# The end of layer 1: ring-buffer operands, sums of two chunks on four column groups, and the order of the projection halves

## The chip, the cores and the metric

The kernel runs on one core of a Trainium2 chip. The metric is the time of one execution on the device in microseconds (us), the median of several runs. A profiled execution also has a span, from its first to its last recorded instruction. The engines are named as in the profile: PE is TensorE (PEld its weight loads), DVE is VectorE, ACT is ScalarE, POOL is GpSimd, SP is SyncE, which here only issues DMAs; "SPq" and "ACTq" rows are DMA issues by SP and ACT.

## The reference, cut to what matters

Two layers work on an array of 2 x 256 x 64 x 64 float32 numbers. Layer 0 is a normalised attention with a gate, and the change doesn't touch it. Layer 1 is softmax attention with four heads of 64 over 4096 positions, an output projection, a bias and a residual:

```
qkv = einsum('oc,bchw->bohw', w_qkv, x) + b_qkv
q, k, v = split(qkv.reshape(b, 4, 192, h*w), 3, axis=2)
attn = softmax(einsum('bhdn,bhdm->bhnm', q, k) / sqrt(64), axis=-1)
out = einsum('bhnm,bhdm->bhnd', attn, v).reshape(b, c, h, w)
return einsum('oc,bchw->bohw', w_out, out) + b_out + x
```

The reshape takes the (4096, 64) result of a head as it lies in memory for 64 rows of 4096. So 512 positions of a head are 8 whole rows of the projection's input, and the projection of any block of 512 columns needs some rows from every block of positions.

## The kernel before

Layer 1 (`L750` on) is cut into 32 units `(b, g, j)`: batch, pair of heads, block of 512 queries. A unit has 32 chunks of 128 keys, in two groups of 16 (`GS`). For each chunk PE makes the scores of both heads (`score`, L878: 128 x 1024 in PSUM), DVE keeps a running maximum (L895) and ACT copies the scores to a ring of 26 SBUF buffers `raw` (`keep`, L896). When a group is through, its maxima are turned by PE (`turn_max`, L903), reduced by DVE (`fold`, L920), written to DRAM as `neg` and read back, spread over all partitions, as `row` (L923, L927). ACT puts the row in PSUM (`place_shift`, L940). From then on, 11 steps (`LAG`) behind the scores, DVE adds the shift to each chunk (`shift`, L948), ACT takes the exponential (`weigh`, L960), and PE multiplies with the values into `av` (`gather`, L982). The sums of the exponentials are made by POOL, one addition to `acc` a chunk (L972); in the last 22 chunks of all (`on_tensor`) most chunks are summed by PE instead, with a product by ones for each single chunk (L992, into `late_sums`). Chunks 10, 11, 12 and 13 of the last unit and all later odd ones go to PE.

A step is two chunks. A list `extras` says what else is hung into a step, at which place in it (`start`, `early`, `early end`, `late`, `late end`, `end`). `seq` keeps the order of the compute instructions on each engine as the code emits them; DMAs on SP keep an order of their own, and each waits at the head of the queue for what it needs. `END` is the step after the last scores. What follows it, steps `END` to `END + 17`, is the drain: no scores any more, only shift, exponential and product of the last 22 chunks, then the last unit's rows.

The last unit's end is in this order. `total` (L1012) adds the POOL sums to `late_sums`. ACT copies them (`keep_total`, L1021), PE turns them (`turn_total`, L1049), POOL and DVE make the factors (L1059, L1060, L1066, L1067), PE turns the two groups' `av` copies (L1042), DVE and POOL make the rows (`rows`, L1077, L1084, L1088). The rows go to DRAM in `att` (L1094, one DMA from SP and one from ACT) and come back, 8 rows of 4096 each, as the last rows of `last_att` (L1100).

The output projection of the last batch is done in two halves of the contraction: half 0 with heads 0 and 1 (`att_first`, long done), half 1 with heads 2 and 3 (`last_att`). `project_half` makes for a block of 512 columns two products (L1231) into a pair of PSUM banks; DVE adds bias and residual after half 0 (L1237) and the rest after half 1 (L1241), both into `x_last`. Half 0 of blocks 0 to 7 is hung into steps of the drain by `FILL`: blocks 0, 1, 2 at its start, 3 to 7 after the last chunk. Half 1 follows for all eight blocks at the very end, each with its store (L1288). `last_output` (L1212) hands the ring's memory to a pool `tail` and loads into it the other rows of `last_att` (L1221) and blocks 5, 6, 7 of the residual `x_last` (L1225); so these loads wait until the ring is no longer used.

Of the kernel before, what the change touches and what calls it, by code (L numbers as in the profile page):

```python
# [14 lines left out]
P = 128  # L15
# [11 lines left out]
def conv_attention_kernel(  # L27
# [740 lines left out]
    with (  # L768
        tc.tile_pool(name="l1", bufs=2) as l1,
        tc.tile_pool(name="psp", bufs=2, space=PSUM) as psp,  # L770
# [4 lines left out]
        own_ring = ExitStack()  # L775
        ring = own_ring.enter_context(tc.tile_pool(name="ring", bufs=2 * LAG + 4))
# [23 lines left out]
        last_att = []  # L800
        first, begun = {}, set()
# [96 lines left out]
        def turn_max(u, n, k):  # L898

            b, g, j = u  # L900
            ps = misc(f"rt_{b}_{g}_{j}_{n}_{k}")
            for i in range(PB):
                seq(nc.tensor.transpose(  # L903
                    ps[:, bass.ts(i, P)], rmax[u, n][:, k, bass.ts(i, P)], ident
                ))
            rts[k] = ps
# [45 lines left out]
        def on_tensor(t):  # L952
            return t >= LATE and (t % 2 == 1 or t < LATE + 4)
# [19 lines left out]

        def gather(t):
# [11 lines left out]
            raws.pop(t - 1, None)  # L986
            if on_tensor(t):
                if u not in srows:
                    srows[u] = psp.tile([P, 2, NB], F32, tag="pair", name="late_sums")[:, 0, :]
                for k in range(2):  # L990
                    r = D1 * n + 32 * k
                    seq(nc.tensor.matmul(  # L992
                        srows[u][r : r + 32, :], ones[:, :32], raws[t][:, k, :],
                        start=r not in begun, stop=False, skip_group_check=True,
                    ))
                    begun.add(r)
# [5 lines left out]
        def total(u):  # L1002


            b, g, j = u
            late = u in srows
            if not late:
                srows[u] = misc(f"sum1_{b}_{g}_{j}")
            for n in range(NG):
                for k in range(2):  # L1010
                    r = D1 * n + 32 * k
                    seq(nc.tensor.matmul(  # L1012
                        srows[u][r : r + 32, :], ones[:, :32], accs[u, n][:, k, :],
                        start=not late, stop=True, skip_group_check=late,
                    ))

        def keep_total(u):
            b, g, j = u
            row = l1.tile([P, NB], F32, tag="kv", name=f"srow_{b}_{g}_{j}")
            if u == units[-1]:  # L1020
                seq(nc.scalar.copy(row, srows[u]))  # L1021
                seq(nc.scalar.activation(losts[u], losts[u], AF.Exp, scale=D1**-0.5))
                srows[u] = row
                return
# [20 lines left out]
        def turn_total(u):  # L1045

            ps = misc("sumt")
            for i in range(PB):
                seq(nc.tensor.transpose(ps[:, bass.ts(i, P)], srows[u][:, bass.ts(i, P)], ident))  # L1049
            s = small.tile([P, NG, 2, PB], F32, tag="sums1", name="sums1_last")  # L1050
            seq(nc.vector.tensor_copy(
                s.rearrange("p n k i -> p i (n k)"),
                ps.rearrange("p (i m e) -> p i m e", i=PB, e=32)[:, :, :, 0],
            ))
            srows[u] = s
# [17 lines left out]
        def rows(u, n):  # L1073
# [6 lines left out]
            last = u == units[-1]  # L1080
# [6 lines left out]
            engine = nc.vector if last else nc.gpsimd  # L1087
            seq(engine.tensor_tensor(r, r, halves.pop(u), ALU.add))  # L1088
# [3 lines left out]
            for k in range(2):  # L1092
                queue = (nc.sync, nc.scalar)[k if last else 0]
                queue.dma_start(  # L1094
# [3 lines left out]
                if last:  # L1098
                    c = ((2 * g + k) * N + j * NB) // D1
                    queue.dma_start(  # L1100
                        out=last_att[0][c % P : c % P + NB // D1, :],
                        in_=att[b][c : c + NB // D1, :],
                    )
# [40 lines left out]
        for n, u in enumerate(units):  # L1144
# [21 lines left out]
            for k in range(NG):  # L1166
                t1 = t0 + (k + 1) * GS // 2
                for i, place in enumerate(("early", "late")):
# [4 lines left out]
            at(t1 + 4, "early", lambda u=u: total(u))  # L1173
            at(t1 + 4, "early end", lambda u=u: keep_total(u))
            at(t1 + 1, "late", lambda u=u: lose(u))
            if u == units[-1]:
                at(t1 + 5, "early", lambda u=u: turn_total(u))
            at(t1 + 5, "late end", lambda u=u: add_sums(u))
            at(t1 + 7, "start", lambda u=u: factors(u))
            for place, k in (("early", 1), ("late", 0)):  # L1180
                at(t1 + 9, place, lambda u=u, k=k: turn_sums(u, k))
                at(t1 + 9, f"{place} end", lambda u=u, k=k: rows(u, k))
# [13 lines left out]
        last_x, first_half = [], []  # L1196

        def fetch_last(i):

            b = B - 1  # L1200
            tag, bufs, pool = (("xb", 3, l1x), ("xo", 1, l1), ("ao", 1, l1))[(i >= 3) + (i >= 4)]
            t = pool.tile([P, CC, NB], F32, tag=tag, bufs=bufs, name=f"x_last_{i}")
            nc.sync.dma_start(out=t, in_=x1[b][i].rearrange("(c p) n -> p c n", p=P))
            last_x.append(t)

        def fetch_first_half():
            for i in range(NJ):
                t = l1o.tile([P, NB], F32, tag=f"k{i}", name=f"att_first_{i}")
                nc.sync.dma_start(out=t, in_=att[B - 1][:P, bass.ts(i, NB)])
                first_half.append(t)  # L1210

        def last_output():  # L1212


            own_ring.close()
            tail = own_tail.enter_context(tc.tile_pool(name="tail", bufs=1))
            b = B - 1
            a = tail.tile([P, N], F32, tag="att", name="last_att")
            for k in range(2):
                r, n = k * D1, D1 - NB // D1  # L1220
                nc.sync.dma_start(out=a[r : r + n, :], in_=att[b][P + r : P + r + n, :])  # L1221
            last_att.append(a)
            for i in range(NJ - 3, NJ):
                t = tail.tile([P, CC, NB], F32, tag=f"xo{i}", name=f"x_last_{i}")
                nc.sync.dma_start(out=t, in_=x1[b][i].rearrange("(c p) n -> p c n", p=P))  # L1225
                last_x.append(t)

        def project_half(j, c, a):
            ps = psp.tile([P, 2, NB], F32, tag="pair", name=f"o1_{c}_{j}")
            for o in range(CC):  # L1230
                seq(nc.tensor.matmul(  # L1231
                    ps[:, o, :], wo1[:, c, bass.ts(o, P)], a, start=True, stop=True
                ))
            for o in range(CC):
                x = last_x[j][:, o, :]
                if c == 0:
                    seq(nc.vector.scalar_tensor_tensor(  # L1237
                        x, ps[:, o, :], bo1[:, o : o + 1], x, ALU.add, ALU.add
                    ))
                else:  # L1240
                    seq(nc.vector.tensor_tensor(x, ps[:, o, :], x, ALU.add))  # L1241

        own_tail = ExitStack()
        for i in range(NJ - 3):
            at(END - 11 + 2 * i, "start", lambda i=i: fetch_last(i))
        at(END, "start", lambda: fetch_first_half())
        at(END + LAG, "late end", lambda: last_output())


        FILL = {  # L1250
            (END, "early end"): (0,), (END + 1, "early"): (1,), (END + 2, "early"): (2,),
# [90 lines left out]
```

## Time and profile before

| what | us |
|---|---|
| median of 3 runs (4685.09 to 4686.68) | 4685.69 |
| the profiled execution's own time | 4685.7 |
| its span | 4683.7 |
| around the span | 2.0 |

| busy in the whole span | PE | DVE | ACT | POOL |
|---|---|---|---|---|
| us | 4505.0 | 3897.1 | 3429.8 | 2515.8 |
| share | 96% | 83% | 73% | 54% |

The shares of the whole span say little about the change, which concerns the last 95 us. What matters there is read from three views: busy time by stretch of the span, the chain of work that ended last (each row: start, duration, what it was), and the timeline (start, duration, engine, line, operation, tile written and read, count, and in brackets the idle time before it with what ended it). A float32 product of 512 columns appears as two records on PE.

### The profile page before, as it was taken

The page shows a single profiled execution, that of the slowest core. Times are in us where ns is not written, and L with a number is a line of the kernel's source. Part 1 is how long each engine was busy: PE and PEld are TensorE (multiplying, and loading weights), DVE is VectorE, ACT ScalarE, POOL GpSimd, SP SyncE. Part 2 cuts the span into 40 slices and gives each one's busy share as a digit, 9 for nine tenths or more (in the row PEclk, how much of TensorE's full clock was granted, in tenths as well). Part 3 has the DMA queues.
Part 4 walks back from the last instruction along what each step waited for, and adds up shares of the span by engine and source line. Part 5 has one row for each costly group of instructions (what it writes and reads, how often), then busy time and mean ns, then how long its engine had stood idle before and what let it go on. Part 6 is the DMA issues. An engine that isn't in the chain of part 4 may idle for free. (4 is left out here: it accounts for less than half of the span.)

```text
span 4683.7 us, 70880 instructions
## 1 busy us (share of the span) xinstructions
PE 4505.0 (96%) x27286; PEld 1512.7 (32%) x27286; DVE 3897.1 (83%) x4505; ACT 3429.8 (73%) x4587; POOL 2515.8 (54%) x1310
## 2 busy tenths in 40 slices
PE   8999999999999999989999999999999999999998
PEld 3433333333333333333333333333333333223222
DVE  6777777777777777449999999999999999999996
ACT  3366666666666666668888888888888888888884
POOL 5300000000000000009999999999999999999994
PEclk9999999999999999999999999999999999999999
DMA  3100000000000000121111221111211112211213
GB/s 100 39 4 20 19 20 15 15 15 17 15 15 15 15 13 13 44 72 35 39 37 39 59 46 39 33 41 43 68 39 38 38 37 64 52 46 39 48 46 99
DMA packets 199166, 174.70 MB, mean 37 GB/s; under 512 B 121124, under 2 KB 121956, under 8 KB 198700
## 3 DMA queue, kind: packets, MB, share of 16 engines
q1 hardware_dynamic: 197020, 169.58, 14.2%
q8 instruction: 214, 3.51, 0.3%
q14 instruction: 124, 1.02, 0.1%
q10 hardware_dynamic: 1808, 0.59, 0.1%
HBM read 127.65 MB, written 42.48 MB: 36 GB/s over the span
## 5 line engine op out<-in xcount | busy, mean ns | idle before, releaser
L972 POOL TENSOR_TENSOR acc<-acc,raw 128x1024 f32<-128x1024 f32 x883 | 2095.2, 2373 | 77.8 <-ACT raw L960 16.1
L402 DVE TENSOR_REDUCE mx<-a 128x1 f32<-128x512 f32 x2048 | 1314.8, 685 | 449.5 <-PE a L398 448.5
L439 ACT ACTIVATE p<-s 128x512 f32<-128x512 f32 x2048 | 1107.9, 595 | 702.1 <-PE a L398 369.3
L878 PE MATMUL s<-q,k 64*128 64x512 f32 x4096 | 1120.9, 637 | 125.8 <-ACT raw L896 117.3
L948 DVE TENSOR_TENSOR raw<-raw,shift 128x1024 f32<-128x1024 f32 x1024 | 1235.1, 1210 | 2.9 <-ACT shift L940 1.4
L895 DVE TENSOR_TENSOR rmax<-s,rmax 128x1024 f32<-128x1024 f32 x960 | 1169.6, 1218 | 74.3 <-PE s L878 67.9
L436 PE MATMUL s<-q,kT 32*128 32x512 f32 x4096 | 1218.1, 640 | 0.0
L896 ACT COPY raw<-s 128x1024 f32<-128x1024 f32 x1024 | 1034.5, 1010 | 207.5 <-DVE rmax L895 161.8
L960 ACT ACTIVATE raw<-raw 128x1024 f32<-128x1024 f32 x1024 | 1085.3, 1060 | 136.2 <-DVE raw L948 103.6
L398 PE MATMUL a<-kT,q 32*128 32x512 f32 x4096 | 1129.5, 643 | 1.4 <-DVE mx L402 1.3
L982 PE MATMUL av<-raw,v 128*64 128x512 f32 x4096 | 993.0, 605 | 1.0 <-ACT raw L960 1.0
L451 PE MATMUL av<-p,v 128*32 128x256 f32 (+1 forms) x7904 | 650.1, 399 | 0.6 <-ACT avs L465 0.6
L878 PEld LDWEIGHTS s<-q,k 64*128 64x128 f32 x4096 | 314.5, 185 | 858.3 <-ACT raw L896 600.7
L501 POOL TENSOR_TENSOR f<-f,dyn 128x16 f32<-128x16 f32 x15 | 3.3, 221 | 1027.4 <-DVE f L500 1027.4
L436 PEld LDWEIGHTS s<-q,kT 32*128 32x128 f32 x4096 | 397.2, 183 | 425.8 <-issue 392.6
L451 PEld LDWEIGHTS av<-p,v 128*32 128x32 f32 x7904 | 157.8, 108 | 751.3 <-issue 737.1
L982 PEld LDWEIGHTS av<-raw,v 128*64 128x64 f32 x4096 | 247.7, 136 | 467.7 <-issue 348.5
L552 POOL TENSOR_SCALAR res<-res 128x1024 f32<-128x1024 f32 x16 | 16.7, 1044 | 659.9 <-ACT res L551 659.9
L398 PEld LDWEIGHTS a<-kT,q 32*128 32x128 f32 x4096 | 305.1, 183 | 31.5 <-DVE mx L402 18.2
L970 POOL TENSOR_TENSOR acc<-raw,raw 128x1024 f32<-128x1024 f32 x64 | 152.7, 2385 | 123.7 <-ACT raw L960 123.7
L920 DVE TENSOR_REDUCE negs<-rt 128x4 f32<-128x512 f32 x128 | 88.2, 689 | 51.1 <-PE rt L903 51.1
L306 DVE RECIPROCAL std<-std 128x128 f32<-128x128 f32 x64 | 56.1, 920 | 39.0 <-ACT std L301 39.0
(328 smaller groups left out, 1848.5 us busy)
## 6 DMA issues: line engine op xcount, KB each, us to landing
row<-neg SPq DMA_DIRECT2D x128, 256.0 KB
x<-in_x_dram SPq DMA_DIRECT2D x16, 512.0 KB
res<-in_x_dram SPq DMA_DIRECT2D x16, 512.0 KB
x<-res SPq DMA_DIRECT2D x16, 512.0 KB
att<-rows SPq DMA_DIRECT2D x63, 128.0 KB
kd<-k1s SPq DMA_DIRECT2D x24, 256.0 KB
vd<-v1s SPq DMA_DIRECT2D x24, 256.0 KB
k<-kd SPq DMA_DIRECT2D x24, 256.0 KB
```

The lines of the kernel that those rows point to most:

```text
L398: seq(nc.tensor.matmul(ps, qs0[u][r, bass.ts(i, P)], kTs[b][r, bass.ts(m, NB)], start=True, stop=True,))
L402: seq(nc.vector.tensor_reduce(mxs[u][:, i * H + h, m : m + 1], ps, AX.X, ALU.max))
L436: seq(nc.tensor.matmul(ps, kTs[b][r, bass.ts(m, P)], qs0[u][r, :], start=True, stop=True))
L439: seq(nc.scalar.activation(pt[:, k, :], ps, AF.Exp, scale=D0**-0.5))
L451: seq(nc.tensor.matmul(avs[u][32 * h : 32 * h + 32, cols], vs0[b][:, m, 32 * h : 32 * h + 32], pts[t, h // 2][:, h % 2, cols], start=(m == ...
L878: seq(nc.tensor.matmul(ps[:, k, :], ks[b, g, m // PB][r, bass.ts(m % PB, P)], qs1[u][r, :], start=True, stop=True,))
L895: seq(nc.vector.tensor_tensor(rmax[u, n], ps, before, ALU.max))
L896: seq(nc.scalar.copy(raw, ps))
L948: seq(nc.vector.tensor_tensor(raws[t], raws[t], shifts[u, t % NM // GS], ALU.add))
L960: seq(nc.scalar.activation(p, p, AF.Exp, scale=D1**-0.5))
L972: seq(nc.gpsimd.tensor_tensor(accs[u, n], accs[u, n], p, ALU.add))
L982: seq(nc.tensor.matmul(avs1[u, n][k * D1 : (k + 1) * D1, :], v[:, m % PB, k, :], raws[t][:, k, :], start=(m % GS == 0), stop=(m % GS == GS ...
```

## The change

Eight things are changed, all in or just before the drain of the last unit; every other instruction keeps its place on its engine.

1. The ring stays open. The residual's blocks 5 to 7 and the other rows of the last half (`att_last`, four tiles of 1024 columns in place of `last_att`) are loaded into ring buffers, from `END + 3` on. The buffers they take are those of chunks 6 to 12 of the last unit.
2. The last group's maxima are turned at once, eight transposes into one PSUM pair, and both reductions follow each other; the two `neg` writes are then issued together and the two `row` reads together.
3. `on_tensor` takes chunks 10, 11, 14, 15, 18, 19, 22, 23, 26, 27, 29, 30, 31 for PE. Two chunks are summed in one go on four column groups (`late_sums`: partitions 0, 32, 64, 96), the first group of chunks in one bank and the second in the other. POOL has 12, 13, 16, 17, 20, 21, 24, 25, 28.
4. `last_lost`: the factor between the two groups (POOL L933 before, ACT L1022) moves from steps `END + 9` (POOL) and `END + 12` (ACT) to step `END + 1`.
5. The first group's sums (`keep_late`, `turn_late`, `add_late`) and rows (`first_rows`) are made during the second group's chunks.
6. The second group's end: one copy of the sums ahead of that of `av`, both turned, two additions, a reciprocal, one addition of rows, and then for each head a product and a bias addition on 128 x 256 (`last_rows`). A head's rows are written as soon as they are ready, by SP for the first and ACT for the second, and come back in four reads of 8 x 1024 on each queue in place of one of 8 x 4096.
7. Half 0 of blocks 3, 4, 5 stays in PSUM and half 1 is accumulated on it; half 0 of 6 and 7 uses two single banks.
8. Half 1 goes in the order 3, 4, 5, 0, 1, 2, 6, 7, on three PSUM pairs in place of two.

```diff
-        own_ring = ExitStack()
-        ring = own_ring.enter_context(tc.tile_pool(name="ring", bufs=2 * LAG + 4))
+        tc.tile_pool(name="ring", bufs=2 * LAG + 4) as ring,
...
         def turn_max(u, n, k):
-            ps = misc(f"rt_{b}_{g}_{j}_{n}_{k}")
+            if (u, n) == (units[-1], NG - 1):
+                if k == 0:
+                    late["turns"] = psp.tile([P, 2, NB], F32, tag="pair", name="last_turns")
+                ps = late["turns"][:, k, :]
+            else:
+                ps = misc(f"rt_{b}_{g}_{j}_{n}_{k}")
...
         def on_tensor(t):
-            return t >= LATE and (t % 2 == 1 or t < LATE + 4)
+            return t >= LATE and (t // 2 % 2 == 1 or t == 2 * END - 3)
...
+        def late_sums(of):
...
+            for k in range(2):
+                for i in range(2):
+                    if of[i] is None and (i == 1 or n == 1 and t != 2 * END - 3):
+                        continue
+                    p = raws[of[i]] if of[i] is not None else accs[u, n]
+                    r = D1 * i + 32 * k
+                    seq(nc.tensor.matmul(
+                        late["sums"][r : r + 32, n, :], ones[:, :32], p[:, k, :],
+                        start=(n, r) not in begun, stop=True, skip_group_check=True,
+                    ))
+                    begun.add((n, r))
...
         def gather(t):
-            if on_tensor(t):
...
+            if on_tensor(t) and t % 2 == 1 and t != 2 * END - 1:
+                late_sums((t - 1, t) if on_tensor(t - 1) else (None, t))
+            elif t == 2 * END - 2:
+                late_sums((t, t + 1))
...
+        def last_lost(u):
+            lose(u)
+            seq(nc.scalar.activation(losts[u], losts[u], AF.Exp, scale=D1**-0.5))
+        def keep_late(n):
+            late["row"] = l1o.tile([P, NB], F32, tag=f"k{n}", name=f"late_row_{n}")
+            seq(nc.scalar.copy(late["row"], late["sums"][:, n, :]))
+        def turn_late(n):
+            ps = late["turned"] = misc(f"late_turned_{n}")
+            for i in range(PB):
+                seq(nc.tensor.transpose(
+                    ps[:, bass.ts(i, P)], late["row"][:, bass.ts(i, P)], ident
+                ))
+        def add_late(u, n):
+            if n == 0:
+                seq(nc.vector.tensor_copy(s, turned[:, 0, :, :, 0]))
+            else:
+                seq(nc.vector.tensor_tensor(s, late["s"], turned[:, 0, :, :, 0], ALU.add))
+            seq(nc.vector.tensor_tensor(s, s, turned[:, 1, :, :, 0], ALU.add))
+            if n == 0:
+                seq(nc.vector.tensor_tensor(s, s, losts[u], ALU.mult))
+            else:
+                seq(nc.vector.reciprocal(s, s))
+        def first_rows(u):
+            r = late["rows"] = l1.tile([P, 2, PB, D1], F32, tag="rows", name="rows_last_0")
+            seq(nc.vector.tensor_tensor(r, avs1.pop((u, 0)), weighted(losts[u]), ALU.mult))
+        def last_rows(u):
+            seq(nc.vector.tensor_tensor(r, avs1.pop((u, 1)), late["rows"], ALU.add))
+            for k in range(2):
+                queue = (nc.sync, nc.scalar)[k]
+                seq(nc.vector.tensor_tensor(r[:, k], r[:, k], f[:, k], ALU.mult))
+                seq(nc.vector.tensor_tensor(r[:, k], r[:, k], bias[:, k], ALU.add))
+                queue.dma_start(
+                    out=to[2 * g + k, bass.ts(j, NB), :].rearrange("(i q) d -> q i d", q=P),
+                    in_=r[:, k, :, :],
+                )
+                for i in range(NJ // 2):
+                    queue.dma_start(
+                        out=last_att[i][c % P : c % P + n, :, :].rearrange("p i n -> p (i n)"),
+                        in_=att[b][c : c + n, bass.ts(i, 2 * NB)],
+                    )
...
+                at(END + 1, "late", lambda u=u: last_lost(u))
+                at(END + 4, "early", lambda u=u: late_sums((None, None)))
+                at(END + 4, "early end", lambda u=u: keep_late(0))
+                at(END + 5, "early", lambda u=u: turn_late(0))
+                at(END + 5, "early end", lambda u=u: add_late(u, 0))
+                at(END + 6, "early", lambda u=u: turn_sums(u, 0))
+                at(END + 6, "early end", lambda u=u: first_rows(u))
+                at(END + LAG, "late", lambda u=u: turn_late(1))
+                at(END + LAG, "late", lambda u=u: add_late(u, 1))
+                at(END + LAG, "late", lambda u=u: turn_sums(u, 1))
+                at(END + LAG, "late", lambda u=u: last_rows(u))
...
-        at(END, "start", lambda: fetch_first_half())
-        at(END + LAG, "late end", lambda: last_output())
-        FILL = {
-            (END, "early end"): (0,), (END + 1, "early"): (1,), (END + 2, "early"): (2,),
-            (END + GS // 2 + 4, "early end"): (3, 4), (END + GS // 2 + 9, "early end"): (5,),
-            (END + GS // 2 + 9, "late end"): (6, 7),
-        }
+        for i in range(NJ // 2):
+            at(END + 3 + i // 2, "start", lambda i=i: fetch_second_half(i))
+        for i in range(EARLY, NJ):
+            at(END + 5, "start", lambda i=i: fetch_first_half(i, l1o, f"k{i}"))
+        for i in range(5, NJ):
+            at(END + 5 + (i - 5) // 2, "start", lambda i=i: fetch_last(i, ring, "raw", None))
+        FILL = {(END, "early end"): 0, (END + 1, "early"): 1, (END + 2, "early"): 2}
...
+                    if c - 2 * LAG - 2 == 2 * END - 2:
+                        keep_late(1)
...
-        for j in range(NJ):
-            project_half(j, 1, last_att[0][:, bass.ts(j, NB)])
+        for j, of in zip(range(EARLY, EARLY + 3), ("pair", "shift", "pair")):
+            ps = bank_pair(f"o1_{j}", of)
+            last_half(j, 0, ps)
+            last_ps[j] = ps
+        for j in range(EARLY + 3, NJ):
+            whole_half(j, 0, "singles")
+        order = [*range(EARLY, EARLY + 3), *range(EARLY), *range(EARLY + 3, NJ)]
+        for n, j in enumerate(order):
+            if j in last_ps:
+                last_half(j, 1, last_ps[j])
+                add_half(j, last_ps[j], True)
+            else:
+                whole_half(j, 1, ("pair", "shift", "pair")[n % 3])
             nc.sync.dma_start(
                 out=out[B - 1, :, bass.ts(j, NB)].rearrange("(c p) n -> p c n", p=P),
                 in_=last_x[j],
             )
-        own_tail.close()
```

`EARLY` is 3. `weighted(f)` spreads a factor over the 64 columns of a head, `fetch_second_half(i)` loads rows 0 to 55 of both heads for 1024 columns into a ring buffer, `fetch_last` and `fetch_first_half` now take the pool and tag to load into, `last_half` issues the two products of a block and half, `add_half` the two DVE additions behind them (L1237's form where the bias is due, L1241's otherwise), and `whole_half` both. In the built program ACT's exponential of chunk 13 stands behind the new ACT exponential of `last_lost`, which waits for POOL's subtraction, and that stands on POOL behind the addition of chunk 12 and the bias addition to the rows of the unit before. On SP, the eight loads of `att_last` and the three of `x_last` stand behind the two writes of the rows of the unit before and ahead of the last unit's write.

## The prediction

> **What bounds the kernel now.** I first read the busy time by stretch over the last 95 us (engine columns: busy us and number of records; then the granted PE clock, DMA share, GB/s):
>
> ```profile
> core 0: us, PE busy (x) PEld busy (x) DVE busy (x) ACT busy (x) POOL busy (x), PEclk, DMA share, GB/s
> 4589.00:4612.00 23.00, 21.47 (x84) 6.47 (x84) 18.23 (x23) 11.86 (x13) 13.22 (x8) 1.00 0.23 47
> 4612.00:4638.00 26.00, 25.04 (x112) 5.59 (x112) 18.17 (x16) 18.65 (x19) 17.98 (x9) 1.00 0.00 1
> 4638.00:4663.00 25.00, 13.08 (x36) 5.33 (x32) 9.23 (x15) 0.69 (x2) 1.88 (x4) 0.79 0.67 158
> 4663.00:4683.70 20.70, 15.55 (x32) 6.56 (x32) 10.31 (x16) 0.00 (x0) 0.00 (x0) 0.91 0.54 203
> ```
>
> The reader is to see three stages. From 4612 to 4638 PE is full, the others have 7 us to spare, and the DMAs carry nothing. From 4638 to 4663 no engine is full and the DMAs carry 158 GB/s. From 4663 PE works again. Then the chain of work that ended last (start, duration, what), which says what the middle stage waits for:
>
> ```profile
> 4634.99 1.87 PE av L982 x8
> 4636.86 0.55 PE late_sums L992 x2
> ...
> 4638.80 13.25 DMA x_last<-x
> ...
> 4653.58 0.61 DVE rows L1077
> ...
> 4654.28 0.70 DVE rows L1088
> 4654.98 0.02 issue
> 4655.01 2.56 DMA att<-rows
> ...
> 4657.71 5.34 DMA last_att<-att
> 4663.05 0.09 issue
> 4663.14 15.57 PE o L1231 x32
> ```
>
> The last products release the ring at 4637.87, only then the loads of `x_last` start, DVE stands in its order at the addition into block 5 until 4652.05, and the last rows are behind that addition. They are written at 4655.01, read back by 4663.05, and then half 1 is made. SP's waits say the same: the load of `last_att` (L1221) stood 29.4 us for the product by ones of L992. Last the timeline of PE:
>
> ```profile
> 4575.85 1.26 PE L1012 MATMUL sum<-acc,ones 128*32 128x512 f32 x8
> ...
> 4646.57 1.88 PE L1231 MATMUL o<-att_first,wo 128*128 128x512 f32 x4
> 4653.64 3.78 PE L1231 MATMUL o<-att_first,wo 128*128 128x512 f32 x4 [5.18 <-DVE x_last L1237]
> 4663.14 15.55 PE L1231 MATMUL o<-last_att,wo 128*128 128x512 f32 x32 [5.72 <-DMA last_att<-att]
> ```
>
> The first row is eight records on four column groups in 1.26 us (1.19 in the chain): four groups run side by side, where the pairs of L992 take 0.98 us for one chunk's four records. The others show the clock: a block costs 1.88 us, but 3.78 after 5.18 us of idleness, and the 32 records after 5.72 us begin with four at about 0.85 us each before they take 1.72 a block.
>
> **The change part by part.** The sums go against the profiled execution: span 4683.7, time 4685.7, which is the median of the runs.
>
> *Up to the second group's shift.* Before, DVE's first shift of chunk 16 is at 4611.98, behind `place_shift`. Afterwards the eight transposes start at 4592.75, as the four did, but block 0's products now take the other PSUM pair and wait for ACT's copy of the last scores (until 4593.8). I carry on with the rows' durations (shift 1.14, exponential 1.07, L1237's pair 1.40, rows 0.69, two chunks of `av` 1.87, two chunks of sums 0.98): exponential 12 ends at 4603.5. Behind it on ACT comes the new wait: the last unit's factor needs POOL's subtraction (0.21), queued behind the addition of chunk 12 (2.38) and the bias addition (1.27), so it is ready at 4607.5 and not at 4603.5. Queued behind it on ACT are exponentials 13 and 14 and `place_shift`, and for those PE's products and DVE's chunk 16 wait. DVE would in any case bring chunks 14 and 15 only at 4608.2 and 4609.3, so the wait costs 0.6: `place_shift` ends at 4611.05. The row is there: its second read was issued at 4603.96 and landed by 4610.83 (6.87 at most); now it is issued at about 4599.4, at the latest landed at 4606.3. Gain 0.9, part of the next sum.
>
> *The drain.* Here PE bounds. Before, 16 chunks cost 8 x (1.87 + 0.98) = 22.8, from 4614.97 to 4637.87. Afterwards av of chunk 16 starts at 4615.0, because the sums of chunks 14 and 15 and of POOL's first group (0.98 + 0.86) stand before it. Then 8 x 1.87, five pairs of sums at 0.98 and two turns of 0.49 make 20.8, plus 0.5 of waiting for exponential 23 behind the first group's DVE work (0.57 + 0.69, of which 0.75 is a wait for the turn). Result 4636.3; call it T. Gain **1.6**. DVE has 18.2 + 1.3 + waits, ends at 4631.8; ACT 17 + 1.2, at 4632.9; POOL's last addition at 4632.2, 0.3 before PE asks for it. So this cover is thin: every us by which POOL is later is a us later for T.
>
> *The loads.* The readers of the buffers taken are chunks 6 to 12, done by 4606. SP reaches the loads after the rows of the unit before (written at 4608.8, 1.3 later than now); eleven issues of 0.35 later all are under way, and the same 3.4 MB as now (13.25 us) are in by 4630. They lie beside the drain, which has no DMA traffic; the shift takes 1.21 us in the first stretch (DMA share 0.23) and in the second (0.00), so I charge nothing for company. Without that cover they would cost what they cost now. The last write is behind these issues on SP, but 24 us later. Half 0's loads for blocks 0 and 1 now stand on SP behind the store and load at 4573.7 and 4576.7 and about the sums at 4578.6 to 4581.5; PE wants them at 4593.8 and 4598. So nothing for them either; without that cover PE waits for each us.
>
> *From T to the write.* The sums' copy (0.58) runs beside the last product. Then: turn (0.65), two small additions (0.2 each, 0.28 apart), turn of `av` (0.65), addition of rows (0.69), and four operations on 256 columns, which I estimate at 0.43 each from 0.69 for 512 and 0.20 for 8, 0.5 apart where one needs the other. ACT's write is issued at T + 4.55 = 4640.85. Before, 4655.01 - 4637.87 = 17.14. Gain **12.6**, the greatest term.
>
> *Write and read back.* Before 8.05: 2.70 until ACT could issue the read, then 5.34. The write stays. Block 3 needs the second of four reads on each queue, so one more issue (0.53), and then a read of 8 x 4096 bytes per queue, which no row shows. From below 2.27, the shortest wait for any transfer here (SP behind its 64 KB write); from above 5.34 each, one after the other, 10.7. I take 3.0, near the 2 KB `neg` write that let SP go on after 3.09 us, as the pieces are small. Landed at 4640.85 + 2.70 + 0.53 + 3.0 = 4647.1. Gain **1.8**.
> The Trainium skill ("DMA: Bandwidth & Descriptors", Rules for kernel authors) speaks against this cut: many small transfers are to be joined into one, as under 64 KB mostly overhead is paid. With the page's fixed 2.0 us for each, one behind the other, block 3's data would land at 4647.7 by my estimate, 0.6 later than in my sum, and the fourth piece 4 us after that, when block 6 doesn't yet ask for it. The trace has no such pair of reads to decide.
>
> *Cover by half 0.* Five blocks at 1.72 from T + 1.85 keep PE busy until 4646.7. DVE's additions for 6 and 7 free the single banks in time (0.74 each per 0.86). So PE idles 0.4 us, not 5.72, and the slow start goes: half 1 is 8 x 1.72 = 13.76 instead of 15.57. Gain **1.8**. Three pairs of banks bring nothing, since 1.72 a block is PE's own work already. The tail, 4678.71 to 4683.7, stays at 4.99.
>
> Sum: 1.6 + 12.6 + 1.8 + 1.8 = **17.8**. Span 4665.9, time **4668**.
>
> One gap is new: PE idles 2.5 us before product 13. Rows show full speed after 1.2 us of idleness and half after 5.18. If the clock falls there, four records cost 1.7 us more, and PE then waits for ACT anyway: 0 to 1.7.
>
> **The rivals.**
> A, *the read back stays slow*: reads of 5.34 in turn, and PE cold again. Half 1 starts between 4649.5 and 4654.2 and loses 1.8 at the start: 4672 to 4677. For it: the row of 5.34 us for 128 KB is long against 2.7 for the write. Against: each piece is a quarter.
> B, *new waits in the drain*: ACT's wait for POOL, POOL's 0.3 us of slack, DVE's wait for the turn. Each of eight additions by POOL (2.38) that slips costs what it slips; 3 to 8 us: 4671 to 4676.
> C, *the loads are not early*: a buffer is held until the last chunk, so block 6's addition on DVE waits until 4652 and block 3 stands behind it on PE: 4652.5 + 15.57 + 4.99, time 4675. Against: the readers are chunks 6 to 12.
> D, *slower*: the clock falls in the new gap of 2.5 us and stays at half in the drain and the projections. The drain's 20.8 us and 13 blocks at 1.72 (22.4) double: +43, time 4711. Each us of PE work at half clock costs one, so it decides from 17.8 us (two fifths of that work), and from 27 us it is measurable. Against: in both cold starts of the trace the clock is back after four records.
>
> **How the numbers follow.** Forecast 0.62, around 4668 (4665 to 4670.5: 1 to 2 us for the drain, 2.27 for a read below). A 0.17, B 0.09, C 0.05, D 0.04; 0.03 for a gain above 21 us. The range 4664 to 4675 takes in the forecast and most of A and B. What a measurement can tell from no change is about 0.2%, 9.4 us: faster is below 4676.3. That holds 0.62 + 0.03 + B 0.09, 0.04 of C and 0.14 of A: 0.92. The rest of A and C and 0.01 of D lie within: 0.05; slower is 0.03 of D.
>
> **What would show it.** The loads of `x_last` 5 to 7 issued by 4616 and no wait for them on DVE; av of chunk 31 done near 4636; four-group sums at about 1 us per two chunks; the last write issued 4.5 us behind that; block 3 of half 1 at 4647 after less than 1 us of idleness, with no slow records. It is wrong if PE's first record of half 1 is past 4652, or if ACT or POOL stand for more than 3 us between 4604 and 4633.

## The result, and the profile after

The changed kernel takes **4667.39 us** (median of 6, 4667.17 to 4668.09), the kernel before 4685.43 beside it (4684.65 to 4686.68): 18.0 us less, a ratio of 0.9961 with a 95% interval of 0.9949 to 0.9974. The forecast was 4668.0 in 4664 to 4675. The profiled execution has a span of 4665.7.

First the busy time by stretch of the changed kernel (engine columns: busy us and number of records; then granted PE clock, DMA share, GB/s):

```profile
core 0: us, PE busy (x) PEld busy (x) DVE busy (x) ACT busy (x) POOL busy (x), PEclk, DMA share, GB/s
4589.00:4612.00 23.00, 18.89 (x78) 6.38 (x80) 19.39 (x24) 12.71 (x14) 16.65 (x10) 1.00 0.22 49
4612.00:4637.00 25.00, 24.27 (x132) 6.29 (x128) 18.12 (x21) 18.38 (x20) 14.32 (x6) 1.00 0.47 134
4637.00:4647.00 10.00, 9.77 (x26) 4.35 (x27) 5.10 (x11) 0.00 (x0) 0.00 (x0) 1.00 0.23 53
4647.00:4665.70 18.70, 13.43 (x32) 5.66 (x30) 11.15 (x17) 0.00 (x0) 0.00 (x0) 1.00 0.58 224
```

The stretch of before from 4638 to 4663, in which the DMAs were busiest and PE worked 13 of 25 us, is gone. Its loads are in the second line: 134 GB/s where there was 1. In the third line PE works 9.8 of 10 us, and the granted clock is 1.00 in all four lines, where the stretches of before had 0.79 and 0.91. The chain of work that ended last (start, duration, what) is now PE's own from 4637.85 on:

```profile
4634.09 1.00 PE late_sums L990 x8
4635.09 1.01 PE av L1004 x4
4636.10 0.60 PE late_turned L1067 x4
...
4637.23 0.63 PE turned L1051 x4
4637.85 22.59 PE o L1289 x52
4660.44 0.02 issue
```

The first line is the sums of two chunks side by side: 1.00 us for eight records, where four took 0.98. No DMA stands in the chain any more. The timeline has the transfers and PE's last records:

```profile
4610.74 3.36 SPq L1278 DMA_DIRECT2D att_last<-att  x8
...
4614.20 2.42 SPq L1264 DMA_DIRECT2D x_last<-x  x3
...
4640.33 0.39 ACTq L1104 DMA_DIRECT2D att<-rows_last  x1
...
4642.38 1.61 ACTq L1110 DMA_DIRECT2D att_last<-att  x4
...
4646.53 13.90 PE L1289 MATMUL o<-att_last,wo 128*128 128x512 f32 x32
```

The loads are issued by 4616.6 (before: from 4638.0 on), the last write 4.2 us behind the last `av`, and half 1 starts without a bracket: PE waited for nothing.

### The profile page after: what moved, and what is told of

It reads as the page before. It is cut to its first block, busy times and chain, and to the rows that moved or that the text cites. A ratio compares the mean times of both kernels' runs of the same rounds, so it can differ in the third digit from the quotient of the medians.

```text
span 4665.7 us, 70910 instructions
## 1 busy us (share of the span) xinstructions
PE 4496.5 (96%) x27290; PEld 1511.0 (32%) x27290; DVE 3894.2 (83%) x4506; ACT 3429.5 (74%) x4588; POOL 2513.9 (54%) x1306
```

## The experiments

The experiments ran later, on two chips, and there the work before the change takes longer: the last score product ends at 4590.2 in the first profile of the changed kernel, at 4606.5 in a second one. The kernel before took medians of 4691.31, 4700.55 and 4701.56 beside them. On one of these chips the two medians of the changed kernel alone differ by 3.8 us, so each run is read from the last score product on, in its own trace. There the three profiles of the changed kernel agree within 0.2 us in each length, apart from one effect told below. The lengths follow one another, in us: from the end of the last score product to DVE's first shift of chunk 16, from there to the end of the last `av`, from there to the start of half 1, half 1 itself, and from its end to the end of the span.

| kernel | to shift 16 | to the end of `av` | to half 1 | half 1 | tail | sum |
|---|---|---|---|---|---|---|
| before | 21.60 | 24.88 | 26.28 | 15.55 | 5.01 | 93.32 |
| after | 20.34 | 25.59 | 10.43 | 13.90 | 5.27 | 75.53 |
| after_again | 20.33 | 26.08 | 10.60 | 13.97 | 5.21 | 76.19 |
| after_third | 20.36 | 25.60 | 10.43 | 13.90 | 5.23 | 75.52 |
| e1_loads_alone | 21.59 | 24.88 | 18.02 | 15.53 | 5.25 | 85.27 |
| e2_loads_late | 20.35 | 25.57 | 24.11 | 16.80 | 5.16 | 91.99 |
| e2b_loads_behind | 20.34 | 26.31 | 25.37 | 14.92 | 5.18 | 92.12 |
| e3_single_sums | 20.86 | 28.56 | 10.44 | 13.90 | 5.26 | 79.02 |
| e4_no_cover | 20.32 | 26.08 | 10.25 | 17.05 | 5.25 | 78.95 |
| e5_plain_halves | 20.34 | 26.45 | 10.89 | 13.95 | 5.21 | 76.84 |
| e6_adds_later | 18.48 | 25.55 | 10.43 | 13.90 | 5.20 | 73.56 |
| e6b_adds_lost_later | 18.49 | 25.56 | 10.43 | 13.92 | 5.26 | 73.66 |
| e8_turns_apart | 21.08 | 25.59 | 10.43 | 13.90 | 5.26 | 76.26 |
| e9_lost_later | 20.25 | 25.58 | 10.44 | 13.90 | 5.21 | 75.38 |

My theory was the sum of the prediction: PE bounds the drain, the early loads and the shorter way of the rows make most of the gain, and half 0 covers the read back. The rivals were that all of it is the loads (or none), that the drain is bound elsewhere, and that the new waits cost.

**One part alone: the loads.** In the kernel before (the last read in four pieces goes with it and isn't shown here):

```
-        own_ring = ExitStack()
-        ring = own_ring.enter_context(tc.tile_pool(name="ring", bufs=2 * LAG + 4))
+        tc.tile_pool(name="ring", bufs=2 * LAG + 4) as ring,
...
-        at(END + LAG, "late end", lambda: last_output())
+        for i in range(NJ // 2):
+            at(END + 3 + i // 2, "start", lambda i=i: fetch_second_half(i))
+        for i in range(NJ - 3, NJ):
+            at(END + 5 + (i - 5) // 2, "start", lambda i=i: fetch_ring(i))
```

> The kernel before, with one part of the change alone: the ring pool stays open, and the other rows of last_att (four tiles of 1024 columns, so the last read comes in four pieces) and x_last 5 to 7 are loaded into ring buffers from step END+3 on. Sums, row turns, order of the rows and of the halves are those of before. My theory (the loads are only part of the path; the work in between is the rest): av and sums end at 4637.9 as before, DVE adds into block 5 at 4647.5 and not at 4652.2, so the last write is issued at 4650.3 and not at 4655.0, the first piece is back some 5.7 us later at 4656.0, and half 1 takes 13.8 to 15.6 and the tail 5.0: span 4675 to 4677, time 4677 to 4678.6, a gain of 7 to 8.5. Rival (all of the gain is the loads, the rest of the change is hidden anyway): 4667 to 4669. Rival (the loads were hidden behind the write anyway): 4684 to 4686.

Measured: 4682.64 against 4691.31 (ratio 0.9984, 0.9974 to 0.9993), 8.7 less; by the table 8.05. Its chain:

```profile
4646.01 1.41 DVE x_last L1238 x2
...
4652.09 0.70 DVE rows L1087
...
4652.82 2.56 DMA att<-rows
...
4655.44 2.99 DMA att_last<-att
4658.43 0.09 issue
4658.52 15.54 PE o L1232 x32
```

The sums ended at 4641.48, so the write is issued 11.3 us behind them instead of 17.1: 5.8 of the gain. The small pieces are back after 2.99 us, where the 128 KB took 5.34. The read back is 2.4 shorter (5.70 from write to half 1, 8.13 before), and that is the pieces, not the loads; the tail is 0.2 longer. So even the loads and the pieces together are worth less than half of 17.8, and both rivals fall.

**The change without its early loads.**

```
-        tc.tile_pool(name="ring", bufs=2 * LAG + 4) as ring,
+        ring = own_ring.enter_context(tc.tile_pool(name="ring", bufs=2 * LAG + 4))
...
+                at(END + LAG, "late", lambda: load_late())
                 at(END + LAG, "late", lambda u=u: turn_late(1))
```

> The changed kernel without its early loads: the ring is closed after the last products, as before, and last_att (one tile, two loads) and x_last 5 to 7 are loaded into a pool in its place; all else is the change. My theory: the loads are issued from 4636.2 on and the last one lands 10 to 13 us later; SP's write and reads of the last rows stand behind them on SP, and DVE's additions of blocks 6 and 7 wait, so half 1 starts at 4650 to 4652 instead of 4646.5, from an idle PE (1.8 more): time 4671.5 to 4675. Rival (with half 0 as cover the place of the loads doesn't matter any more): 4667 to 4668.5. Rival (the loads are the whole gain): 4680 or more.

Measured: 4688.98 against 4691.31 (ratio 0.9997, 0.9987 to 1.0006), and 16.5 above the changed kernel in the table, not 4 to 8. I had left out what the trace shows first (timeline of SP, ACT, DVE and PE):

```profile
4641.07 0.77 SPq L1323 DMA_DIRECT2D last_att<-att  x2
...
4641.88 14.54 SPq L1266 DMA_DIRECT2D x_last<-x  x3
...
4645.16 0.39 ACTq L1105 DMA_DIRECT2D att<-rows_last  x1
...
4656.14 1.52 ACTq L1111 DMA_DIRECT2D last_att<-att  x4
4656.35 1.41 DVE L1289 SCALAR_TENSOR_TENSOR x_last<-o,bo,x_last 128x512 f32<-128x512 f32 x2 [11.22 <-DMA x_last<-x]
4656.52 0.44 SPq L1105 DMA_DIRECT2D att<-rows_last  x1
4657.15 3.62 PE L1280 MATMUL o<-att_first,wo 128*128 128x512 f32 x4 [7.59 <-DVE x_last L1289]
```

ACT's write of 128 KB, issued beside the loads, takes 10.88 us in the chain; in e4, below, without them, it takes 1.99. And the third load of `x_last` stands 7.2 us on SP for that write, with SP's own write behind it. So the rows wait for the loads even though ACT issues them from another queue. The Trainium skill ("DMA: Bandwidth & Descriptors", Issuing engines are not separate DMA queues) says that DMAs of all engines run on the same 16 DMA engines and interleave; the 10.88 us agree.

The write isn't all of it. The DVE and PE lines above show that block 6's addition waits for its own late load, and that PE's last block of half 0 stands behind it, until 4660.8. Half 1 starts at 4665.04. So with the loads where they are, a prompt write could have brought it 4.3 us forward and no more; the rest of the 16.5 is the late loads and the slow clock behind the idle time.

I tried to part the loads' own time from their place ahead of the write:

```
                 at(END + LAG, "late", lambda u=u: last_rows(u))
+                at(END + LAG, "late", lambda: load_late())
```

> As e2_loads_late, but the late loads stand behind SP's last write in the program (one of the two loads of last_att behind the write, x_last 5 to 7 behind the reads of the last rows). In e2 half 1 started 24.1 us behind the last av and ACT's write of the last rows took 10.9 us beside the loads, against 2.0 in the changed kernel without its cover. Theory (a small write issued behind large loads waits for them, so the loads' place before the write is the larger part of the loss): ACT's write takes 2 to 3 us again, the additions into blocks 6 and 7 wait for x_last until some 17 us behind the last av, and half 1 starts at 16 to 19 instead of 24: 6 to 9 above the changed kernel. Rival (it is the loads' own time, wherever they stand): again 23 to 25, 15 to 17 above it.

Measured: 4697.78 against 4701.56 (ratio 0.9993, 0.9984 to 1.0002); half 1 starts 25.4 behind `av`, so my figure failed. SP issued one 896 KB load 3.3 us ahead of its write all the same and the other 0.3 us ahead of ACT's write, whose reads follow 8.8 us behind it. And the loads of `x_last`, now behind the reads (from 4667.6 on), became the longer wait: by the chain ACT's read that block 3 needs has landed by 4668.3, 16.6 behind `av`, but block 6's addition stands until 4672.7 and PE behind it:

```profile
4672.72 1.41 DVE L1290 SCALAR_TENSOR_TENSOR x_last<-o,bo,x_last 128x512 f32<-128x512 f32 x2 [16.79 <-DMA x_last<-x]
```

So late loads cost by their own time and by holding up the write, and these two causes aren't parted; a write with no load in flight beside late loads wasn't tried. What is shown: without early loads the rest of the change brings 1.3 us over before (91.99 against 93.32), with them 17.8. Neither part does it alone.

**PE or another engine in the drain.**

```
-                late_sums((t - 1, t) if on_tensor(t - 1) else (None, t))
+                if on_tensor(t - 1):
+                    one_sum(t, 1)
...
+            elif on_tensor(t) and t % 2 == 0 and t != 2 * END - 2:
+                one_sum(t, 0)
```

> The changed kernel, but the sums of two chunks no longer stand side by side on four column groups: the even chunk's sums follow its own av, the odd chunk's its own, so each pair of chunks costs two turns on two groups. Chunk 29 with the accumulator stays on four groups. My theory (PE bounds the drain): five pairs from chunk 14 on cost 1.96 instead of 1.00, 4.8 us in all, less some 0.9 us in which PE waits in the drain of the changed kernel: T moves from 4636.1 to 4640 to 4640.9 and the time to 4671 to 4672.2. Rival (ACT, DVE or POOL bound the drain, PE's gain is paper): 4667.4 to 4668.4.

Measured: 4675.25 against 4691.31 (ratio 0.9967, 0.9956 to 0.9979); 3.5 above the changed kernel by the table, of which 3.0 from shift 16 to the end of `av`. Its chain in the drain is PE without a break from 4622.26 on:

```profile
4622.91 1.01 PE av L1021 x4
4623.93 0.98 PE late_sums L1002 x4
4624.91 1.01 PE av L1021 x4
4625.91 0.98 PE late_sums L1002 x4
4626.90 0.59 PE turned L1071 x4
4627.49 2.73 PE av L1021 x12
```

PE bounds, and the rival (0 to 1) falls. But 3.5 is below my 3.9 to 4.8, as I had counted one pair too many: chunk 15's sums run beside those of POOL's first group (records from 4619.06 and 4619.07 on), so behind shift 16 only four pairs cost more, 3.9 in all. PE's idle time from there to the end of `av` falls from 1.3 us in the changed kernel to 0.4, which leaves the 3.0; the other 0.5 comes before shift 16, where the pair of chunks 10 and 11 stands. The changed kernel's chain goes through POOL's last additions (from 4624.64) and ACT: its drain is bound by PE and POOL almost together.

**When the rows are back.**

```
-        for j, of in zip(range(EARLY, EARLY + 3), ("pair", "shift", "pair")):
-            ps = bank_pair(f"o1_{j}", of)
-            last_half(j, 0, ps)
-            last_ps[j] = ps
-        for j in range(EARLY + 3, NJ):
-            whole_half(j, 0, "singles")
```

> The changed kernel without half 0 of blocks 3 to 7 (their output lacks the first half's product and the bias): PE stands idle from 4637.9 until the rows written last are back, so that the trace shows when that is. Block 3 asks first, for the second of four pieces on each queue; ACT issued that piece's read at about 4642.9. My theory (small pieces, 3.0 us from issue): half 1 starts at 4645.9, the first four records cost about 0.85 each for the idle time, half 1 takes 15.6, the tail 5.2: span 4666.7, time 4668 to 4669.5. By the fixed 2.0 us of the Trainium skill's page DMA: Bandwidth & Descriptors, one behind the other, the start is 4646.4 by estimate and the time 0.5 more. Rival (a piece takes as long as the 128 KB of before, 5.34, one after the other): start 4653, time 4675 to 4677. The order of the halves gained 1.8 if the time is that much above the changed kernel's; if the time is the same, half 0 as a cover bought nothing but its own place.

Measured: 4676.42 against 4691.31 (ratio 0.9970, 0.9958 to 0.9981). From the timeline:

```profile
4646.38 0.39 ACTq L1104 DMA_DIRECT2D att<-rows_last  x1
...
4647.56 1.30 SPq L1110 DMA_DIRECT2D att_last<-att  x4
4648.44 2.03 ACTq L1110 DMA_DIRECT2D att_last<-att  x4
...
4652.40 17.05 PE L1289 MATMUL o<-att_last,wo 128*128 128x512 f32 x32 [8.49 <-DMA att_last<-att]
```

and from the chain, ACT's issue of the second piece and the transfer that ended last:

```profile
4649.06 0.27 ACTq L1110
...
4649.42 2.98 DMA att_last<-att
```

PE's bracket names the read, so the data of block 3 are there 6.0 us after ACT's write and 10.25 after the last `av`; PE asks for them 10.43 after it. The cover holds, by 0.2 us. The reads begin 2.06 behind the write (I took 2.70), and PE starts 3.3 after the second piece's issue at 4649.06 (3.0). The chain puts the end of the wait down to the piece issued after it, so 3.3 is the most that the second piece took. Counted from the last `av` of the changed kernel that is 4646.35, where I had 4645.9. My estimate from the page (the Trainium skill, "DMA: Bandwidth & Descriptors", Anatomy of one DMA — SWDGE (gpsimd) path) was 4646.4, and the start agrees with it, but the working behind it doesn't hold. The first piece on ACT in e1 took 2.99 us and not 2.0; and in e4 no byte moves from 4651.3 to 4652.4, while four reads of 2.0 us one behind the other on SP, from 4647.56 on, would last until 4655.6. The reads overlap. Besides, the page fits its 2.0 us to DMAs that GpSimd issues, and these come from SP and ACT. Half 1 takes 17.05, not 15.6: an idle time of 8.5 us costs 3.2 on PE's clock.

**The order of the halves.**

```
+        for j in range(EARLY, NJ):
+            whole_half(j, 0)
+        for j in range(NJ):
+            whole_half(j, 1)
```

> The changed kernel with the halves of the last blocks as they were: half 0 of blocks 3 to 7 is added to x at once, half 1 runs over the blocks 0 to 7, and both use the two PSUM pairs alone. My theory (1.72 us a block is PE's own work, three pairs of banks and held halves bring nothing): DVE frees the pair of block 3 some 0.6 us after PE asks for it, the rest follows in step, and half 1 starts at most 0.6 later: time 0 to 0.7 above the changed kernel's. Rival (with 1.4 us of DVE for each of ten more halves DVE falls behind and PE stands between the blocks, or block 0's data are later than block 3's): 2 to 4 above.

Measured: 4683.36 against 4700.55 (ratio 0.9969, 0.9956 to 0.9981; after_again 4684.45, 0.9966). Half 1 starts 10.89 behind `av`: 0.3 to 0.5 later, from one wait in PE's timeline and what follows it. The held halves are worth that much here, and the rival falls. (The longer drain is the clock, below.)

```profile
4651.55 3.60 PE L1289 MATMUL o<-att_first,wo 128*128 128x512 f32 x8
4655.53 5.47 PE L1289 MATMUL o<-att_first,wo 128*128 128x512 f32 x12 [0.39 <-DVE x_last L1298]
4660.84 13.95 PE L1289 MATMUL o<-att_last,wo 128*128 128x512 f32 x32
```

**The start of the drain.** First the two turns apart again (`places = ("early", "late")`, and both in the single bank):

> The changed kernel with the two turns of the last maxima one behind the other in the single bank again, the second one at its old place, so that the second row of the shift is read back later. My theory (the row isn't what the shift waits for: place_shift asks at 4609.3, the row is there): shift 16 0 to 0.3 later, time the same. Rival (the turns ahead are needed, or the row lands late): 1 to 3 later.

Measured: 4683.74 against 4701.56 (ratio 0.9964, 0.9950 to 0.9978; after_third 4680.65). Shift 16 comes 0.74 later, between theory and rival: DVE stands 0.74 us for the second turn, and its order carries that on. The row isn't late. Then the lost factor two steps later (`at(END + 3, "late", lambda u=u: last_lost(u))`):

> The changed kernel, but the last unit's lost factor (POOL's subtraction and ACT's exponential) stands two steps later, so that exponentials 13 and 14 no longer stand behind POOL. My theory: ACT's wait of 3.9 us disappears, PE's gap of 2.1 us before product 13 with it or moves, but DVE brings chunk 15 only at 4609.2 and the shift's bank is free only then: time 0 to 0.3 under the changed kernel's. Rival (the new wait is a real cost, 0.6 by my sum, up to 2): 0.6 to 2 under it.

Measured: 4682.58 against 4700.55 (ratio 0.9964, 0.9951 to 0.9976); shift 16 only 0.09 earlier. ACT's wait is there in the changed kernel (3.91 us for POOL) and costs 0.1. Then DVE's own order:

```
+        for (t, place), j in {(END, "early end"): 0, (END + 1, "early end"): 1, (END + 2, "end"): 2}.items():
+            at(t, place, lambda j=j: add_half(j, later.pop(j), True))
```

> The changed kernel, but on DVE the additions of half 0 into blocks 1 and 2 stand later than their products: block 1's behind the shift of chunk 12 and the first rows of the unit before, block 2's behind the shift of chunk 15; the products stay where they are. In the changed kernel DVE stands 2.3 us between 4596 and 4609 for these products and for the second turn, and the shift of chunk 16 (4610.5) is behind it. My theory (DVE's order sets the start of the drain, and the drain is PE's): shift 16 about 1.8 earlier, T as well, time 1.2 to 2 under the changed kernel's. Rival (ACT's wait for POOL's lost, or the row, sets the start): 0 to 0.4 under it.

Measured: 4680.37 against 4700.55 (ratio 0.9959, 0.9946 to 0.9971; after_again 0.9966), and shift 16 at 18.48 instead of 20.34. DVE's timeline of the changed kernel, then of this one:

```profile
4599.83 1.41 DVE L1298 SCALAR_TENSOR_TENSOR x_last<-o,bo,x_last 128x512 f32<-128x512 f32 x2 [1.45 <-PE o L1289]
...
4603.83 0.69 DVE L1135 TENSOR_TENSOR rows<-turned,f 128x512 f32<-128x512 f32 x1 [0.87 <-issue]
...
4610.51 3.48 DVE L951 TENSOR_TENSOR raw<-raw,shift 128x1024 f32<-128x1024 f32 x3 [1.28 <-ACT shift L943]
```

```profile
4618.71 3.47 DVE L951 TENSOR_TENSOR raw<-raw,shift 128x1024 f32<-128x1024 f32 x3
4622.10 1.40 DVE L1298 SCALAR_TENSOR_TENSOR x_last<-o,bo,x_last 128x512 f32<-128x512 f32 x2
4623.42 3.47 DVE L951 TENSOR_TENSOR raw<-raw,shift 128x1024 f32<-128x1024 f32 x3
```

The addition that stood before the last shifts now fills the time in which ACT places the shift, and the wait of 1.28 is gone. By the table this kernel is 1.97 us under the changed one; its median is 4.1 under on the same chip, but the intervals of the ratios overlap. With e9's edit as well:

> The changed kernel with both of the late placements: the additions into blocks 1 and 2 as in e6, and the lost factor two steps later as in e9. Expected from the last score product to the end of the span: e6 took 73.56, and ACT's wait for POOL of 3.9 us and PE's gap go with it: 73.2 to 73.6, that is 2 to 2.5 under the changed kernel, and no half clock before shift 16.

Measured: 4679.56 against 4701.56 (ratio 0.9958, 0.9944 to 0.9973; after_third 0.9959), 73.66 by the table: no further gain.

**The reference runs.**

> The changed kernel as it is, as a reference on the chip on which the next three run. It should stand 17 to 19 us under the kernel before, whatever the chip's own run-up takes.

> The changed kernel as it is, as a reference beside the next three; from its last score product to shift 16 some 20.3 us, from there to the end of av 25.6 or 26.1 (the latter where the granted clock falls to half in PE's gap of 2.1 us), from there to the end 29.6 to 29.8.

Measured: 0.9966 (0.9953 to 0.9978) and 0.9959 (0.9945 to 0.9973), 16.1 and 20.9 under before. They differ in the drain, 26.08 against 25.60. In the gap of 2.1 us before product 13 the first of them lost its clock. The gap, the products behind it and the next us in after_again, then the same gap and products in after (us, five engines, granted clock, DMA share, GB/s):

```profile
4622.82:4624.94 2.12, 0.00 (x1) 0.01 (x1) 2.12 (x3) 1.21 (x3) 2.10 (x3) 1.00 0.00 0
4624.94:4628.40 3.46, 3.46 (x9) 0.92 (x11) 2.20 (x3) 3.17 (x4) 2.37 (x1) 0.51 0.34 83
4628.40:4629.40 1.00, 1.00 (x10) 0.19 (x9) 1.00 (x2) 0.76 (x1) 0.00 (x0) 1.00 0.88 291
```

```profile
4606.46:4608.57 2.11, 0.00 (x1) 0.00 (x0) 2.11 (x3) 1.21 (x3) 2.11 (x3) 1.00 0.00 0
4608.57:4610.60 2.03, 2.02 (x8) 0.40 (x8) 0.74 (x2) 2.03 (x3) 2.00 (x1) 1.00 0.46 114
```

The same program with the same gap runs at half clock for 3.4 us in one execution and at full speed in the other. Of the eight profiles with this gap four show the drop (after_again, e2b, e4, e5), each with a drain 0.5 to 0.9 longer; e3, e6, e6b and e9, with a gap of 1.5 or less, show none. The last section says what parts the four from the others.

## Why the prediction was right, term by term

| term | predicted gain | measured | from |
|---|---|---|---|
| up to shift 16 | 0.9 | 1.26 | 21.60 to 20.34 |
| up to the end of the drain, with it | 1.6 | 1.56 | 47.49 to 45.93 behind the last score product |
| to ACT's write | 12.6 | 12.9 | 17.14 to 4.23 |
| write and read back, until half 1 starts | 1.8 | 1.9 | 8.13 to 6.20 |
| half 1 | 1.8 | 1.65 | 15.55 to 13.90 |
| tail | 0 | -0.26 | 5.01 to 5.27 |
| sum | 17.8 | 17.8 | 93.32 to 75.53 |

The greatest term holds, and the runs part it: 5.8 of its 12.9 come with the early loads alone (e1), the other 7.1 with the shorter way of the rows. That split goes by the order in which the parts are added: in e2, with late loads, ACT's write is issued just as early (4.2 behind `av`), but it then takes 10.88, and SP's write is issued only 15.6 behind `av`. So the shorter way of the rows pays little without the early loads.

Within the terms some steps were off:

- "Without that cover they would cost what they cost now" was far too small. Late loads cost 16.5 us with the new order of work and not 4 to 8, as the last write then waits among them and block 6's addition waits for its own load.
- ACT's wait for POOL was costed at 0.6 and costs 0.1 (e9). DVE's order sets shift 16, as said, but the two turns made together save 0.74 of DVE's time (e8), which I had not counted.
- The drain proper gained less than the 0.7 left of my 1.6, namely 0.3: from shift 16 on PE also waits for ACT and POOL, whose thin cover I had named. That the two terms still add up to my 1.6 is luck: the first was 0.4 too small, the second 0.4 too large.
- The read back: 6.0 us by e4 against my 6.23. The write was shorter than the 2.70 taken, the piece at most a little longer than 3.0; the two errors partly cancel. So the rows are back before PE has done its half 0, and the 6.20 of the table ends with PE's own work, without the 0.4 of idleness that I had. The write of 2.27 us that I took as the lower bound moves 128 KB, not 64.
- Half 1 gained 0.15 less than summed, and the tail lost 0.26 that I had at nothing. The total met to 0.1 is partly such errors of both signs.
- The clock: the new gap's 0 to 1.7 was bounded rightly, 0 in four profiles and 0.5 to 0.9 in four; that the profile of the result is one of the first four is luck. Rival D's lasting half clock didn't come. But what I held against it was misread: the clock was not back after four records in both cold starts of before. It stood at half from 4652.7 to 4666.3, through the first, the idle time behind it, and the four slow records of the second. The price of a cold start was taken as 1.8; after 8.5 us of idleness it is 3.2 (e4).
- "Three pairs of banks bring nothing" is nearly right: with the held halves they bring 0.3 to 0.5 (e5).

Rival A falls (half 1 starts at 4646.53 without a wait), B with the 0.1 that ACT's wait costs and the end of `av` at 4636.10 (forecast 4636.3), and C with the loads issued by 4616.6.

## What to carry to other kernels

Load the operands of a tail before its last small write: here late loads didn't only arrive late, they also held up the write and the read back that the tail waits for. Removing one of two waits on such a path may show little until the other goes too (8 us for the loads with the smaller reads, 1.3 for everything but the loads, 17.8 together). An engine with idle time can still set the pace by its order: moving two additions on DVE behind shifts that others wait for was worth 2 us in the trace.

## What the runs showed of the hardware

The granted clock falls and returns in stretches of 3.4 us or multiples. By the clock records of the traces, half clock lasted 3.41 us in e1 (PE idle 4.7) and in after_again (2.1), 6.83 at the start of half 1 in e2 (4.3), 10.24 in e4 (8.5) and 13.65 in before, over two idle times. The Trainium skill ("TensorE: Matmul & The Clock Gate", What's actually happening) gives a free-running window of 3413 ns; these lengths agree with it. The same page (Why this matters for your kernels) advises against idle gaps above about 3 us. Here a gap of 2.1 us was enough in four of eight profiles; the measurement decides.

What parts the four can be worked out. Count windows of 3.413 us (a quarter of the 13.65) back from each profile's last change of the clock, and take PE's idle share of each. In the four profiles with the drop the gap lies within one window (in e5 all but 0.02 us of it), and PE is idle for 61 to 62% of that window (in after_again 4621.57 to 4624.98, where the clock falls). In the other four the end of a window cuts the gap, and no window is idle for more than 42%. Windows idle for 50% (e3, e9) bring no drop either. The clock came back at the end of a window with PE busy for 92% or more (before, e1, e2), and not after one with 82% (e4, behind the 8.5 us). So the same idle time costs more or less by where it falls.

ACT's 128 KB write took 1.99 us in e4, with only SP's like it beside it, 8.74 in e2b beside 1.8 MB of loads and 10.88 in e2 beside some 2.8 MB. A read of 128 KB in one piece took 5.34 us on ACT's queue in before, its first quarter 2.99 in e1.

What made the work before the change up to 16 us longer in the experiments, in both kernels, stays open.
